# A new table of steps, and later constants issued behind the first query, in a software-pipelined graph attention + Mamba2 + GRU + MoE kernel

## The chip, the cores and the metric

The kernel runs on one core of one Trainium2 chip. The core has five engines that work side by side, each on its own instructions in order: PE (TensorE, matrix products, with its weight loads listed apart as PEld), DVE (VectorE), ACT (ScalarE), POOL (GpSimd) and SP (SyncE, which here only issues DMAs). They wait for each other through semaphores. The metric is the device time of one execution in microseconds (us), as the median of several runs.

## The reference, cut to what matters

The input is `x` of 32 elements x 512 tokens x 256 features and, for each element, an adjacency matrix of 512 x 512. All arithmetic is in 32-bit floats. Two layers are computed, each with a residual sum:

```python
# layer 0
x = x + gat(layernorm(x), adj, W, a)        # leaky_relu(f1_i + f2_j), mask, softmax, times W h
x = x + mamba2_block(layernorm(x), ...)     # x @ W_in, conv of 4, silu, scan over time, gate, norm, W_out, W_lin
# layer 1
x = x + gru_cell(gat1(adj, layernorm(x)), layernorm(x))
x = x + moe(layernorm(x))                   # shared MLP + the best 2 of 4 experts
```

In the attention, the score of a pair of tokens depends on one number of each of the two tokens (`f1`, `f2`). No step mixes two elements.

## The kernel before, in words

One element is 4 tiles of 128 tokens (T=4). The work on one element is cut into 21 parts, listed in `PARTS`: `load_x`, `load_adj`, `gnn0` (the attention of layer 0), `mamba` (its layer norm), `steps_of_time`, `decays_of_states`, two halves of `convolution`, `products_of_bc`, `gate_of_z`, `scan`, `output`, `load_adj` again, `gnn1` (the attention of layer 1), two halves of `gru` (m=0 and m=1), `gru_out`, `moe`, `gates`, `experts` and `mixture`. Each part is a Python generator: it issues a few instructions, yields, and goes on at its next turn.

What sets the order of all instructions is a table written out by hand, `PLAN`: for each part, the turn of each of its steps. Element b adds b times `PERIOD` (428) to its turns; all steps of all elements are sorted by turn and issued in that order, and no scheduler changes it afterwards. 428 is also the number of steps of one element, so a turn is a place in the order and not a time. In the steady state some four to five elements are in flight: while `gnn0` of one element runs, `scan` of the element before, `gnn1` and `gru` of one further ahead and `experts` of another are interleaved with it. Each engine takes its own instructions strictly in that order; so an instruction that waits holds up everything behind it on its engine.

The names that matter below:

- `attention` (L277 on; used by `gnn0` and `gnn1`): DVE takes the largest `f2` (`top`), PE transposes it (`ps_top`, L287), DVE and ACT make 8 rows of factors `fewT` (L300, L302), SP writes them to DRAM as `line` (L305) and reads them back, spread over all partitions, as `query` (L308, 512 KB). ACT (L320) and DVE (L323, L326, with the adjacency tile `adj`) turn `query` into the unnormalised scores `pT`, two tiles at a time. PE multiplies them in `gnn0` (`ps_h`, L356) or `gnn1` (`ps_g`, L692).
- The issuing of DMAs: all of them are issued by SP, in one queue. At the start the constants are loaded: the tables of layer 0 first, then those of later parts from `woutT` (L130) to `gb`. Inside the loop, SP issues per element the loads of `x` and twice of four `adj` tiles, `rows` and twelve `ecs` for the scan, `gates` and four `pg` for the experts, `line` and `query` of both attentions, and the output. Eight semaphores are used in turn for DMAs, so a DMA also waits for the eighth before it.
- `steps_of_time`: PE sums the decays (`ps_E`, L441), DVE makes `byS`, `byL` and `byHL` (L444, L446, L456), PE multiplies these (`ps_seg`, L464), ACT makes the decay tables `L` (L470, L473).
- `gru`: PE sums two products for each gate (`ps_rz`, L718 and L721), and `ps_hn` and `ps_in` (L743); ACT makes `gate`, POOL subtracts (L751, both operands 128x512), DVE finishes with L753 and L755 (`oT`). `gru_out` has PE transpose `oT` (`ps_o`, L764), and DVE adds it to `x`.
- `mamba`: after the layer norm, POOL adds `blin` to `x` (L376, 128x1024). `output` sums squares (L653, `ps_ss` L665) and multiplies with `wc`, a product of `woutT` and `wlin` that is made once, by `prepare_output` (L215 on), ahead of the first element's `output`. That preparation is the first user of the constants of later parts.

Of the kernel before, what the change touches and what calls it, by code (L numbers as in the profile page):

```python
# [11 lines left out]
F32 = mybir.dt.float32  # L12
# [6 lines left out]
P = 128  # L19
N = 512  # L20
T = N // P
D = 256
KD = D // P
HEADS = 8
NP = HEADS // 2
HD = 64
# [5 lines left out]
def adj_ffn_kernel(ctx: ExitStack, tc: tile.TileContext, i: dict, out: bass.AP):  # L32
    nc = tc.nc
# [47 lines left out]
    def load(name, shape, src):  # L81
        t_ = const.tile(shape, F32, name=name)
        nc.sync.dma_start(t_, src)
        return t_

    def kchunks(ap):
        return ap.rearrange("(k p) o -> p k o", p=P)
# [18 lines left out]

    we = const.tile([P, KD, D + 1], F32, name="we")
    nc.sync.dma_start(we[:, :, :D], kchunks(i["L0_gnn_W"]))  # L110
    first = Element(0)
# [14 lines left out]
    dskip = load("dskip", [P, NP], i["dskip"])  # L126
    normw = load("normw", [P, NP], i["norm_w"])
    blin = load("blin", [P, D], i["L0_ffn_b_lin"].partition_broadcast(P))
    woutT = quad("woutT", KD)
    nc.sync.dma_start(woutT, kchunks(i["woutT"]))  # L130
    wlin = row("wlin").rearrange("p (k d) -> p k d", k=KD)
    nc.sync.dma_start(wlin, kchunks(i["L0_ffn_W_lin"]))
    w1 = row("w1").rearrange("p (k d) -> p k d", k=KD)
    nc.sync.dma_start(w1, kchunks(i["L1_gnn_W"]))
    nc.sync.dma_start(abs_[1], i["L1_gnn_a"].partition_broadcast(P))
    wT = row("wT").rearrange("p (k d) -> p k d", k=KD)
    nc.sync.dma_start(wT, kchunks(i["L1_gnn_WT"]))
    raw = big("raw").rearrange("p t n -> p (t n)")[:, :KD * 3 * D].rearrange("p (k o) -> p k o", k=KD)
    nc.sync.dma_start(raw, kchunks(i["wihT"]))
    whh = load("whh", [P, KD, 3 * D], kchunks(i["whhT"]))  # L140
    bih = load("bih", [P, 6], i["b_ih"])
    bhh = load("bhh", [P, 6], i["b_hh"])
    sw1 = load("sw1", [P, KD, 256], kchunks(i["L1_ffn_sW1"]))
    sb1 = load("sb1", [P, 2], i["sb1"])
    sw2 = load("sw2", [P, 2, P], kchunks(i["L1_ffn_sW2"]))
    sb2 = load("sb2", [P, 1], i["sb2"])
    sw3 = load("sw3", [P, D], i["L1_ffn_sW3"])
    ew1 = const.tile([P, KD, 4, P], F32, name="ew1")
    for e in range(4):
        nc.sync.dma_start(ew1[:, :, e, :], kchunks(i["L1_ffn_eW1"][e]))  # L150
    eb1 = load("eb1", [P, 4], i["eb1"])
    ew2 = load("ew2", [P, 4, HD], i["L1_ffn_eW2"].rearrange("e f g -> f e g"))
    eb2 = load("eb2", [P, 2], i["eb2"])
    ew3 = load("ew3", [P, 2, D], i["ew3"].rearrange("(j p) o -> p j o", p=P))
    b3 = const.tile([P, D], F32, name="b3")
    nc.gpsimd.memset(b3, 0.0)
    for r in range(0, P, 32):
        nc.sync.dma_start(b3[r:r + 4, :], i["L1_ffn_eb3"])
        nc.sync.dma_start(b3[r + 4:r + 5, :], i["L1_ffn_sb3"].unsqueeze(0))
    gw = const.tile([P, KD, 32], F32, name="gw")  # L160
    nc.gpsimd.memset(gw, 0.0)
    nc.sync.dma_start(gw[:, :, :4], kchunks(i["L1_ffn_gW"]))
    gb = load("gb", [P, 4], i["L1_ffn_gb"].partition_broadcast(P))


    slopes = const.tile([P, 3], F32, name="slopes")
# [111 lines left out]
    def attention(e, f21, kind):  # L278

        f2 = f21[:, 0, :]
        top = small.tile([P, 1], F32, name="top")
        nc.vector.tensor_reduce(top, f2, AX.X, ALU.max)
        yield
        pt = bank("ps_top")
        nc.tensor.transpose(pt[:, :P], top.to_broadcast([P, P]), ident)  # L287
        yield
        nf = small.tile([P, 1], F32, name="nf")
        nc.vector.tensor_reduce(nf, pt[:, :P], AX.X, ALU.max, negate=True)  # L290
        yield
        nfs = small.tile([P, 2], F32, name="nfs")
        nc.vector.tensor_scalar_mul(nfs, slopes[:, 0:3:2], nf)
        yield

        pf = bank("ps_f1")
        nc.tensor.transpose(pf[:2 * T, :P], f21[:, 1:, :].rearrange("p u t -> p (u t)"), ident)
        yield
        q8 = small.tile([P, P], F32, name="fewT", bufs=4)[:2 * T, :]
        nc.scalar.activation(q8, pf[:2 * T, :P], AF.Relu, scale=slopes[:2 * T, 1:2], bias=nfs[:2 * T, 1:2])  # L300
        yield
        nc.scalar.activation(q8, q8, AF.Exp, scale=-1.0)  # L302
        yield
        line = dram.tile([2 * T, P], F32, name="line")
        nc.sync.dma_start(line, q8)  # L305
        yield
        query = quad("query", 2)
        nc.sync.dma_start(query.rearrange("p n (t m) -> p (n t) m", t=T), line.partition_broadcast(P))  # L308
        yield
        key1 = small.tile([P, T], F32, name="key1")  # L310
        nc.scalar.activation(key1, f2, AF.Exp, bias=nf)
        key2 = small.tile([P, T], F32, name="key2")
        nc.scalar.activation(key2, f2, AF.Exp, scale=0.2, bias=nfs[:, 0:1])
        yield
        pT = big("pT")

        for j in range(0, T, 2):
            both = [(i, pT[:, i, :]) for i in (j, j + 1)]
            for i, p in both:
                nc.scalar.activation(p, query[:, 0, :], AF.Identity, scale=key1[:, i:i + 1])  # L320
                yield
            for i, p in both:
                nc.vector.scalar_tensor_tensor(p, query[:, 1, :], key2[:, i:i + 1], p, op0=ALU.mult, op1=ALU.max)  # L323
                yield
            for i, p in both:
                nc.vector.scalar_tensor_tensor(p, e.adj[i].bitcast(kind), 2.0 ** -120, p, op0=ALU.max, op1=ALU.min)  # L326
                yield
        return pT
# [558 lines left out]
    def mixture(e):  # L887
# [10 lines left out]
        for t, ps in enumerate(pes):  # L898
# [17 lines left out]

    PERIOD = 428
    PLAN = (
        (51,),
        (0, 99, 106, 135),  # L920
        (82, 83, 84, 86, 87, 88, 89, 91, 101, 102, 110, 111, 113, 114, 118, 119, 120, 121, 131, 138, 139, 144,
         147, 151, 152, 153, 158, 159, 160, 161, 162, 194, 196, 203, 204, 205, 206, 207, 208, 210, 211, 212,
         223, 249, 250, 251, 261, 262, 263, 276, 277, 278, 279, 280, 281, 282, 284, 289, 290, 291, 295),
        (283, 287, 292, 297, 298, 300, 314, 315, 316, 317, 325, 354, 355, 356, 357, 409),
        (525, 526, 532, 545, 551, 552, 595, 596, 597, 598, 599, 600, 601, 602, 603, 604, 605, 614, 616, 617,
         618, 625, 626, 627, 628, 629, 660, 661, 662, 663, 664, 665, 666, 667, 668, 669, 670, 671, 672, 673,
         674, 675, 721, 724),
        (630, 637, 722),
        (381, 382, 383, 384, 394, 395, 398, 412, 413, 457, 462, 464, 467, 469, 470, 476, 477, 480, 485, 518,
         591),  # L930
        (414, 415, 463, 465, 466, 478, 501, 502, 506, 513, 522, 523, 540, 676),
        (425, 426, 543, 555, 556, 557, 558, 583),
        (385, 389, 396, 427, 447, 473, 475, 488, 507, 508, 568, 576),
        (684, 685, 686, 687, 688, 694, 695, 696, 697, 698, 699, 700, 701, 702, 703, 727, 729, 730, 731, 732,
         733, 735, 737, 738, 739, 740, 749, 754, 755, 756, 757, 758, 759, 760, 761, 763, 764, 786, 787),
        (734, 741, 746, 747, 762, 765, 766, 767, 775, 776, 788, 789, 790, 791, 792, 793, 794, 795, 796, 797,
         807, 808, 819, 820, 821, 828, 829, 830, 831, 833, 834, 836, 838, 844),
        (736, 781, 889, 902),
        (285, 832, 835, 839, 845, 846, 847, 848, 857, 858, 859, 860, 861, 862, 863, 864, 865, 866, 867, 868,
         869, 870, 871, 872, 873, 874, 878, 879, 880, 881, 882, 883, 886, 910, 911, 914, 915, 919, 920, 921,  # L940
         922, 923, 924, 925, 926, 927, 928, 931, 932, 933, 937, 948, 949, 959, 961, 965, 972, 981, 982, 989,
         990, 992, 993),
        (909, 917, 918, 1021, 1022, 1034, 1035, 1047, 1048, 1049, 1073, 1074, 1075, 1082, 1083),
        (896, 900, 912, 1013, 1036, 1039, 1040, 1043, 1051, 1077, 1078, 1080, 1085, 1086, 1087),
        (1108, 1109, 1110, 1120),
        (1111, 1121, 1200, 1201, 1206, 1207, 1208, 1226, 1227, 1228, 1229, 1242, 1243, 1244, 1246),
        (1384, 1391, 1416, 1425, 1426, 1427, 1430, 1434, 1438, 1440, 1465, 1466, 1469, 1497, 1498, 1499, 1500,
         1504, 1509, 1512, 1570, 1572, 1624, 1630, 1662),
        (1327, 1380, 1392, 1406, 1429, 1433, 1604, 1606, 1607, 1608, 1625, 1626, 1627, 1633, 1658, 1659, 1660,
         1661),  # L950
        (1681, 1683, 1705, 1706, 1707, 1708, 1732, 1733, 1740, 1743, 1744, 1876),
    )
    order = sorted((b * PERIOD + turn, b, n, k) for b in range(B) for n, turns in enumerate(PLAN)
                   for k, turn in enumerate(turns) if b or n > 1)
# [55 lines left out]
```

## Time and profile before

| what | us |
|---|---|
| median of 3 runs | 3426.61 (3424.37 to 3428.89) |
| profiled execution, its own time | 3430.65 |
| span of the profiled execution | 3428.9 |
| PE busy in the span | 3281.2 (96%) |
| DVE busy | 2917.6 (85%) |
| ACT busy | 1527.9 (45%) |
| POOL busy | 543.4 (16%) |
| one steady period (distance at which PE's groups repeat) | 102.75 |
| PE busy in the first 50 us, in the next 50, in the next 100 | 9.58, 33.02, 87.10 |

The span is the time between the first and the last instruction of the profiled execution; its own time has 1.75 us more around it. The mean granted clock of PE is 0.992. The 32 elements at 102.75 us would be 3288 us; the rest is the filling of the pipeline at the start and its draining at the end. Busy shares are means over the whole span[...].

### The profile page before, as it was taken

What the parts mean: (1) busy time and instruction counts of PE and PEld (TensorE: products, weight loads), DVE (VectorE), ACT (ScalarE), POOL (GpSimd) and SP (SyncE); (2) the same over time, 40 slices, a digit from 0 to 9 for tenths busy, and PEclk for the clock granted to TensorE, in tenths of its full rate; (3) what the DMA queues carried; (4) which work ended last, traced back from release to release, by engine and by line L of the source; (5) the groups of instructions that cost most, each with busy time, mean ns of one, the idle gap of its engine ahead of it and who ended that gap; (6) DMA issues with size and microseconds to landing.
All of it is one profiled execution on the core that took longest, in us unless ns stands there. A gap on an engine that the chain in (4) does not pass through costs nothing.

```text
span 3428.9 us, 48462 instructions
## 1 busy us (share of the span) xinstructions
PE 3281.2 (96%) x16616; PEld 1920.2 (56%) x16616; DVE 2917.6 (85%) x7650; ACT 1527.9 (45%) x3016; POOL 543.4 (16%) x591
## 2 busy tenths in 40 slices
PE   4789999999999999999999999999999999999988
PEld 2455556555556555556555556555556555556554
DVE  4788888988888888888888888988888988888963
ACT  2344444444444444444444444444444444444432
POOL 0111111111111111111111111111111111111110
PEclk9899999999999999999999999999999999999999
DMA  3101111212111212111212111212111212111111
GB/s 120 49 31 61 55 57 51 67 39 67 55 56 51 67 39 67 54 56 52 67 39 67 54 56 51 67 39 67 55 57 49 67 39 67 56 58 48 55 32 37
DMA packets 187983, 190.41 MB, mean 56 GB/s; under 512 B 18884, under 2 KB 145496, under 8 KB 187736
## 3 DMA queue, kind: packets, MB, share of 16 engines
q1 hardware_dynamic: 187736, 187.31, 18.0%
q8 instruction: 132, 2.16, 0.3%
q14 instruction: 115, 0.94, 0.1%
HBM read 166.01 MB, written 21.23 MB: 55 GB/s over the span
## 4 chain that ended last, share of the span: by engine, by line
PE 76%; DVE 11%; issue 6%; DMA 4%; ACT 2%; SPq 1%; POOL 0%; DVEq 0%; ACTq 0%; POOLq 0%
PE ps_g L692 7%; PE ps_e L864 6%; PE ps_conv L493 6%; PE ps_mo L674 6%; PE ps_z L555 5%; PE ps_rz L721 4%; DMA query<-line 4%; PE ps_rz L718 3%; PE ps_y L629 3%; PE ps_h L356 3%; PE ps_in L743 3%; DVE pT L323 3%; PE ps_g L364 3%; PE ps_e L902 3%; PE ps_xT L273 2%
## 5 line engine op out<-in xcount | busy, mean ns | idle before, releaser
L500 DVE SCALAR_TENSOR_TENSOR acc<-ps_conv,cw,acc 128x511 f32<-128x511 f32 (+2 forms) x480 | 348.9, 744 | 16.4 <-ACT acc L497 10.6
L245 POOL TENSOR_TENSOR rstd<-rstd,mhalf 128x4 f32<-128x4 f32 x128 | 129.4, 1011 | 1194.8 <-DVE rstd L243 1038.9
L323 DVE SCALAR_TENSOR_TENSOR pT<-query,key,pT 128x512 f32<-128x512 f32 x256 | 213.9, 876 | 107.9 <-ACT pT L320 107.9
L493 PE MATMUL ps_conv<-xT,win 128*128 128x512 f32 x640 | 300.9, 601 | 0.0
L692 PE MATMUL ps_g<-xn,pT 128*128 128x257 f32 x1024 | 259.9, 392 | 12.4 <-DVE pT L326 12.2
L356 PE MATMUL ps_h<-pT,xn 128*128 128x512 f32 x512 | 237.0, 607 | 23.3 <-DVE pT L326 23.3
L596 POOL TENSOR_TENSOR ecs<-ecs,cc 128x512 f32<-128x512 f32 x96 | 134.0, 1396 | 770.3 <-DVE rs L368 531.0
L692 PEld LDWEIGHTS ps_g<-xn,pT 128*128 128x128 f32 x1024 | 190.4, 192 | 100.4 <-issue 33.9
L555 PE MATMUL ps_z<-xT,win 128*128 128x512 f32 x512 | 242.3, 596 | 0.0
L721 PE MATMUL ps_rz<-go,wih 128*128 128x512 f32 x512 | 238.7, 599 | 0.0
L320 ACT ACTIVATE pT<-query,key 128x512 f32<-128x512 f32 x256 | 172.3, 710 | 148.0 <-DMA query<-line 148.0
L864 PE MATMUL ps_e<-xT,ew 128*128 128x512 f32 x512 | 237.0, 596 | 0.0
L718 PE MATMUL ps_rz<-xT,whh 128*128 128x512 f32 x512 | 235.4, 592 | 0.0
L674 PE MATMUL ps_mo<-wc,xh 128*128 128x256 f32 x1024 | 227.2, 380 | 0.0
L497 ACT ACTIVATE acc<-ps_conv,cb,cw 128x512 f32<-128x512 f32 x160 | 123.9, 774 | 220.8 <-PE ps_conv L493 220.7
L262 DVE TENSOR_SCALAR xn<-x,mv,rstd 128x256 f32<-128x256 f32 (+1 forms) x512 | 215.3, 474 | 6.0 <-POOL rstd L245 5.9
L255 DVE BATCH_NORM_STATS2 st<-x 128x6 f32<-128x256 f32 x512 | 206.2, 420 | 6.6
L674 PEld LDWEIGHTS ps_mo<-wc,xh 128*128 128x128 f32 x1024 | 193.1, 191 | 24.8
L849 ACT ACTIVATE e<-ps_e,eb 128x512 f32<-128x512 f32 x192 | 127.6, 680 | 176.7 <-PE ps_e L864 174.7
L751 POOL TENSOR_TENSOR oT<-xT,gate 128x512 f32<-128x512 f32 x64 | 112.4, 1778 | 581.7 <-ACT gate L748 581.7
L493 PEld LDWEIGHTS ps_conv<-xT,win 128*128 128x128 f32 x640 | 120.2, 192 | 149.3 <-issue 142.7
L657 ACT ACTIVATE sq<-xh 128x512 f32<-128x512 f32 x128 | 79.9, 631 | 255.1 <-DVE xh L653 253.7
(205 smaller groups left out, 6691.6 us busy)
## 6 DMA issues: line engine op xcount, KB each, us to landing
adj<-in_adjT_dram SPq DMA_DIRECT2D x256, 256.0 KB
query<-line SPq DMA_DIRECT2D x64, 512.0 KB
ecs<-rows SPq DMA_DIRECT2D x384, 64.0 KB
x<-in_x_dram SPq DMA_DIRECT2D x32, 512.0 KB
pg<-gates SPq DMA_DIRECT2D x128, 128.0 KB
out_dram<-x SPq DMA_DIRECT2D x32, 512.0 KB
rows<-fewT SPq DMA_DIRECT2D x32, 64.0 KB
gates<-fewT SPq DMA_DIRECT2D x32, 64.0 KB
```

The source lines that it names most:

```text
L255: nc.vector.bn_stats(st[:, t, :], x[:, t, :])
L262: nc.vector.tensor_scalar(xn[:, t, :width], x[:, t, :width], mv[:, t, 0:1], r[:, t:t + 1], op0=ALU.subtract, op1=ALU.mult)
L323: nc.vector.scalar_tensor_tensor(p, query[:, 1, :], key2[:, i:i + 1], p, op0=ALU.mult, op1=ALU.max)
L356: nc.tensor.matmul(ps, xn[:, j, k * P:(k + 1) * P], pT[:, j, :], start=j == 0, stop=j == T - 1)
L493: nc.tensor.matmul(ps, win[:, k, 512 + c * P:512 + (c + 1) * P], e.xT[:, k, :], start=k == 0, stop=k == KD - 1)
L500: nc.vector.scalar_tensor_tensor(acc[:, s:], ps[:, :N - s], cw[:, c, 3 - s:4 - s], acc[:, s:], op0=ALU.mult, op1=ALU.add)
L555: nc.tensor.matmul(ps, win[:, k, j * P:(j + 1) * P], uT[:, k, :], start=k == 0, stop=k == KD - 1)
L674: nc.tensor.matmul(ps[:, :D], xh[:, j, t * P:(t + 1) * P], wc[:, j, :], start=j == 0, stop=j == NP - 1)
L692: nc.tensor.matmul(ps[:, :D + 1], pT[:, j, cut], xn[:, j, :], start=j == 0, stop=j == T - 1)
L718: nc.tensor.matmul(ps, whh[:, k, cols], xT[:, k, :], start=k == 0, stop=False)
L721: nc.tensor.matmul(ps, wih[:, k, cols], e.go[:, k, :], start=False, stop=k == KD - 1)
L864: nc.tensor.matmul(ps, ew1[:, k, m, :], vT[:, k, :], start=k == 0, stop=k == KD - 1)
```

## The change

Two things are changed. First, 31 DMAs that load the constants of later parts are no longer issued at the start: `load_later` and `tile_later` only note them on a list, and `attention` issues that list for the first element, directly behind its `query`. Their tiles, sizes and sources stay as they were; together they carry about 4.5 MB. Second, the turns in `PLAN` are new. `PERIOD`, the parts and the number of their steps stay; an element's last turn is 1954 in place of 1876.

```diff
+    later = []
+
+    def load_later(t_, src):
+        later.append((t_, src))
+
+    def tile_later(name, shape, src):
+        t_ = const.tile(shape, F32, name=name)
+        load_later(t_, src)
+        return t_
+
     woutT = quad("woutT", KD)
-    nc.sync.dma_start(woutT, kchunks(i["woutT"]))
+    load_later(woutT, kchunks(i["woutT"]))
...
-    whh = load("whh", [P, KD, 3 * D], kchunks(i["whhT"]))
-    bih = load("bih", [P, 6], i["b_ih"])
+    whh = tile_later("whh", [P, KD, 3 * D], kchunks(i["whhT"]))
+    bih = tile_later("bih", [P, 6], i["b_ih"])
...
-    nc.sync.dma_start(gw[:, :, :4], kchunks(i["L1_ffn_gW"]))
-    gb = load("gb", [P, 4], i["L1_ffn_gb"].partition_broadcast(P))
+    load_later(gw[:, :, :4], kchunks(i["L1_ffn_gW"]))
+    gb = tile_later("gb", [P, 4], i["L1_ffn_gb"].partition_broadcast(P))
...
         nc.sync.dma_start(query.rearrange("p n (t m) -> p (n t) m", t=T), line.partition_broadcast(P))
+        if e is first:
+            while later:
+                nc.sync.dma_start(*later.pop(0))
         yield
```

Of the new table, the rows that are spoken of below (in the order of `PARTS`: `load_x` and `load_adj`, then the second `load_adj`, the two halves of `gru` and `gru_out`):

```diff
-        (51,),
-        (0, 99, 106, 135),
+        (100,),
+        (0, 156, 169, 206),
...
-        (736, 781, 889, 902),
+        (854, 867, 923, 925),
...
-        (909, 917, 918, 1021, 1022, 1034, 1035, 1047, 1048, 1049, 1073, 1074, 1075, 1082, 1083),
-        (896, 900, 912, 1013, 1036, 1039, 1040, 1043, 1051, 1077, 1078, 1080, 1085, 1086, 1087),
-        (1108, 1109, 1110, 1120),
+        (983, 984, 985, 1115, 1116, 1120, 1121, 1122, 1162, 1189, 1207, 1208, 1222, 1223, 1224),
+        (980, 990, 991, 1094, 1095, 1097, 1099, 1100, 1101, 1136, 1137, 1138, 1139, 1140, 1142),
+        (1251, 1252, 1253, 1254),
```

In SP's queue the steady order per element changes with it. Before: `rows`, 12 `ecs`, `adj`, `gates`, 2 `pg`, `adj`, 2 `pg`, `adj`, `line` of `gnn1`, 2 `adj`, `x`, `query` of `gnn1`, 3 `adj`, `line` and `query` of `gnn0`, output. After: `rows`, 12 `ecs`, 3 `adj`, `gates`, 4 `pg`, 2 `adj`, `x`, `line` and `query` of `gnn1`, 3 `adj`, `line` and `query` of `gnn0`, output. Of the two halves of `gru`, before has them interleaved step by step on PE; after finishes m=1 first, and the last gate of m=0 comes later, behind steps of `experts` and `scan` of other elements.

Lines of the changed kernel are numbered one higher from L110 on, 11 higher behind the constants, and 14 higher from L322 on.

## The prediction

> **What bounds the kernel now.** I read the page's busy times and slices first, then the table by stretches of time, then the timeline of the start, the waits, and one period of the timeline in the middle. The page:
>
> ```profile
> PE 3281.2 (96%) x16616; PEld 1920.2 (56%) x16616; DVE 2917.6 (85%) x7650; ACT 1527.9 (45%) x3016; POOL 543.4 (16%) x591
> PE   4789999999999999999999999999999999999988
> DVE  4788888988888888888888888988888988888963
> DMA  3101111212111212111212111212111212111111
> ```
>
> TensorE is busy nearly always, except in the first three slices (85.7 us each) and a little in the last two. The table by stretches says how much (columns after the length: busy us of PE, PEld, DVE, ACT, POOL; granted clock; DMA share; GB/s):
>
> ```profile
> 0.00:50.00 50.00, 9.58 (x19) 4.22 (x20) 15.61 (x57) 6.15 (x11) 3.81 (x18) 1.00 0.64 206
> 50.00:100.00 50.00, 33.02 (x120) 15.91 (x120) 38.36 (x110) 20.02 (x40) 4.60 (x5) 0.81 0.05 14
> 100.00:200.00 100.00, 87.10 (x414) 52.25 (x413) 72.98 (x198) 35.05 (x70) 11.97 (x13) 0.92 0.14 44
> 428.00:856.00 428.00, 421.98 (x2208) 246.98 (x2207) 380.41 (x995) 195.53 (x386) 73.63 (x77) 1.00 0.19 56
> ```
>
> The reader is to see two regimes. In the middle an element costs 102.75 us (the distance after which TensorE's groups repeat), PE busy 98.6% of it: only a shorter or longer hand-off on TensorE's own path counts there, some 29 times over. In the first 200 us PE lacks 70 us; each microsecond by which the first element's chain starts earlier is worth up to one, once. The start in the timeline (start, length; in brackets the idle time before and what ended it):
>
> ```profile
> 20.15 0.31 ACT L302 ACTIVATE fewT<-fewT 8x128 f32<-8x128 f32 x1
> 33.06 0.47 SPq L83 DMA_DIRECT2D gb<-in_L_ffn_gb_dram  x1
> 33.63 0.29 SPq L305 DMA_DIRECT2D line<-fewT  x1
> 35.28 0.34 SPq L308 DMA_DIRECT2D query<-line  x1
> 39.63 2.56 ACT L320 ACTIVATE pT<-query,key 128x512 f32<-128x512 f32 x4 [18.79 <-DMA query<-line]
> 42.46 9.26 PE L356 MATMUL ps_h<-pT,xn 128*128 128x512 f32 x16 [23.27 <-DVE pT L326]
> ```
>
> ACT had the query factors ready at 20.46 us (L302), but SP's queue is in order and still issues constants up to `gb` at 33.06; only then go `line` and `query`, and ACT, DVE and PE stand idle for 19 to 23 us. The waits (total us, times, longest) show the same, and the small stalls of the middle:
>
> ```profile
> ACT pT L320 <- DMA query<-line: 148.0, 34, 18.8
> PE ps_h L356 <- DVE pT L326: 23.3, 1, 23.3
> PE ps_o L764 <- DVE oT L755: 32.6, 31, 2.2
> ```
>
> The first wait happens once per element, but 34 times make 148.0 us, and ACT is 45% busy; only the first, of 18.8 us, passes on to PE (second row). The third is PE's own, about 1.05 us per element. One period's timeline shows its origin:
>
> ```profile
> 1638.41 0.42 PE L441 MATMUL ps_E<-le,dA 128*32 128x128 f32 x8
> 1638.91 0.41 DVE L444 TENSOR_SCALAR byS<-ps_E,kinds 128x128 f32<-128x128 f32 x1 [0.32 <-PE ps_E L441]
> 1639.48 3.49 POOL L751 TENSOR_TENSOR oT<-xT,gate 128x512 f32<-128x512 f32 x2 [16.64 <-ACT gate L748]
> 1639.67 2.16 DVE L456 TENSOR_TENSOR byHL<-byL,head 128x1024 f32<-128x1024 f32 x1
> 1644.12 2.00 PE L464 MATMUL ps_seg<-byHL,byS 32*128 32x512 f32 x16
> 1646.05 3.70 PE L356 MATMUL ps_h<-pT,xn 128*128 128x512 f32 x8
> 1651.39 0.98 PE L764 MATMUL ps_o<-ident,oT 128*128 128x128 f32 x7 [1.02 <-DVE oT L755]
> ```
>
> From the start of `ps_h` to that of the last group is 5.34 us; eight matmuls at 0.43 (the spacing of 512-column records) and one transposition of 0.11 fill 3.55. So the hand-off costs 1.8 us per element. DVE is late because, between `byS` and L755, it has some 10.6 us of work and loses two more to POOL's subtraction (next part).
>
> **What the Trainium skill says.** "SBUF — State Buffer", section "Who interferes with whom": a DVE instruction with two SBUF inputs contends with a GpSimd one that reads SBUF, and the one that came first gets the shared ports for its whole length. The trace agrees: `byHL` takes 2.16 us beside POOL's L751 above, and 1.22 at the shortest of its 32 instances; L890, typically 0.69, takes 2.79 when POOL's L376 (2.35 us) has begun. "DMA: Bandwidth & Descriptors", section "Issuing engines are not separate DMA queues": all transfers run on the same 16 engines, so constants issued behind the query still share them with it if they overtake. The trace: share 0.64 in the first 50 us, 0.19 in the middle. What the two small transfers cost, the trace has itself, from element 1: `line` 89.18 to `query` 90.41 (1.23 us), and `query` to ACT's first use 94.14 (3.73). "Perfetto Trace Analysis", section "Identifying the Most-Contended Engine": matmul busy time is a poor measure of nearness to the limit, because matmuls are pipelined. It agrees: at the fastest spacings seen, an element's TensorE work is 97.5 to 98 us, so 98.6% busy still hides about 5 us of slack per element.
>
> **The change, part by part.**
>
> *Constants behind the query.* 31 DMAs (`woutT` to `gb`, issued 13.81 to 33.53 in before) move behind `query`. The last load that stays, `blin`, is issued at about 11.3, and the first element's arithmetic up to L302 needs none of the moved ones. So `line` goes at about 20.5 (end of L302), `query` 1.23 later at 21.8, ACT's L320 3.73 to 4.35 later (element 1's and element 0's own spacing): 25.5 to 26.1 against 39.63. Gain 13.5 to 14.1 us; I take 13.5. No work on PE covers this idle time, and everything after it in the first element hangs on it. What is late next: (1) the moved constants themselves. They took 19.7 us to issue, so they will be out at about 42 and landed by about 50; the first user is the preparation of `output` (L215) at 115 us, later 101: 50 us of cover. (2) Element 1's `adj` and `x`, behind them in SP's queue: issued at about 43 to 46 instead of 36 to 38, first used by DVE's statistics at 78.10, later about 64.6: 15 us of cover. (3) Bandwidth: the query is issued first, so at worst a part of a microsecond. If PE were saturated in the next 150 us the gain would be eaten; it is idle for 17 us in 50:100 and 13 in 100:200, so I expect it to pass on whole. Bounds: −14.5 to −10.
>
> *`query` of the second attention directly behind `line`.* In before, two `adj` and `x` stand between: for element 0 `line` 162.64, `query` 164.43, use at 171.99, that is 9.35 us, and PE stands about 4 us at `ps_g` 171 to 177. In after, by the order of the two programs, they follow each other: 1.23+3.73 = 5.0 us. Saves 4.4 us of the chain in the fill; part will show as another wait. I take −3 (0 to −5). In the middle of the run this transfer has slack: the wait stands on ACT; PE's share (`ps_g` on DVE's `pT`, 12.2 us in total over 18 times) is 0.4 per element and goes.
>
> *The new table, steady part.* It adds and removes no instruction; it changes positions. On TensorE, before has E, four gate groups (5.2 us), `ps_seg`, `ps_h`, `ps_o`; after puts `ps_o` far behind the last gate, so the 1.8 us goes. Together with `ps_g`: −2.2 us. New, by adding row durations along the new order:
> - From `ps_top` to dA DVE has 5.6 us of steps, TensorE 5.2 to 5.4 of other work: with 0.3 for the hand-over, a stall of about 0.65 ahead of `ps_E`.
> - Between `ps_E` and `ps_seg` TensorE now has only one gate and one `in` group, 3.4 us, in place of 5.2. DVE needs `byS`, `byL`, `byHL`: 0.41+0.40+1.22 and hand-overs. If it is free, 0.15 stall; if POOL's L751 (it becomes ready within 0.1 us of `byHL`) takes the ports first, `byHL` is held, 1.2. I weigh the second 0.7: about 0.9.
> - POOL's L376 now falls beside L755 and L653 of another element, and holds DVE about 2.2 us; with TensorE's work in front of `ps_ss`, 0.8 of it arrives (0.3 to 1.5).
>
> Sum: −2.2 +0.65 +0.9 +0.8 = +0.15 us per element, in truth 0 with an error of 0.7. Over 29 steady elements 0 ± 20 us. Both ends: −1.2 (no collision) to +1.5 (both).
>
> *The end.* An element's own chain becomes 59 places of the order longer (turn 1876 to 1954), which is a depth of places, not time: the last element's chain at the end has 40 us of PE idle in the last 250 us in before. After, a stall of 2.2 us ahead of the gates goes (two more groups stand in front), and a longer run from `pg` to the next matmul costs 1 to 2. I take 0 (−3 to +5).
>
> The sum, against the profiled execution: 3430.65 (span 3428.90 and 1.75 around it) − 13.5 − 3 + 0 + 0 = 3414.2. The median of the runs shown, 3426.61, stands 4.0 below that execution; so 3410, and with the steady +0.15 rounded in part, 3411.
>
> **The rivals.** (B) *Steady shorter too*, by 0.5 to 1.2 us per element: the `ps_o` stall goes and POOL starts its operations at moments when DVE isn't reading two inputs. For it: the gain is visible in two rows of waits. Against: POOL's operations become ready at places where DVE's chains are short of time. It gives 3411 − 29×(0.5 to 1.2) = 3376 to 3396. (C) *Slower side*: the new hand-off ahead of `ps_seg`. POOL's L751 takes the shared ports first in every period, `byHL` waits for it, and with only 3.4 us of TensorE work in front, each such hold is lost whole; L376 adds its own. It turns at 16/29 = 0.55 us per element: beyond that the fill's 16.5 us are used up. At +1.0 it gives 3411+29 = 3440, at +1.5 3454. For it: `byHL` is held already today (2.16 instead of 1.22), hidden by 5.2 us of gates. Against: it needs POOL to win each time by 0.1 us. (D) *The fill gain doesn't arrive*: the constants or element 1's loads come late, or the time is taken back by PE's full queue: then 3424 to 3427, no change. Against: the covers of 15 and 50 us above.
>
> **How the numbers follow.** Forecast A (steady within 0.5 us per element, fill gain arrives): 0.48, own range 3396 to 3426. B 0.25, C 0.22, D 0.05. About 0.2%, 6.9 us, is what a measurement of this kernel can tell from no change: faster is below 3419.8, slower above 3433.5. From A 0.41 are faster and 0.07 within; B is all faster; of C 0.08 are within and 0.14 slower; D is within, 0.04, or slower, 0.01. Sum: 0.66, 0.19, 0.15. For the range, B's lower end beyond 3384 (0.05) and C's beyond 3440 (0.10) are left out, and so it holds some 0.85.
>
> **What would show it.** The timeline of after: `line` at about 20.5, `query` at 21.8, ACT's L334 at 25.5 to 26.1; PE's first `ps_h` at about 29; `x` of element 1 used near 64.6 without a wait on its DMA. The waits: `ps_o` on DVE gone; in its place `ps_E` or `ps_seg` on DVE, and the mean of `byHL` above 1.3 or not, which decides between B and C. The period: 102.75 ± 0.5. Wrong if `query` is used later than 30 us, if the period moves by more than 0.7, or if the last 250 us lose more than 5.

## The result, and the profile after

The changed kernel takes 3459.68 us (median of 4 runs, 3458.51 to 3463.68) against 3426.53 of before in the same session (4 runs): the ratio is 1.0099, with a 95% interval of 1.0081 to 1.0116. It is slower by 33 us; the forecast was 3411, faster. The profiled execution took 3458.51 us, its span is 3456.8. One of the 13 runs of `e5_copy_early` below, 3819.31 us at a granted clock of 0.847, is left out of every comparison.

I read the page again first, then the table by stretches (length; busy us of PE, PEld, DVE, ACT, POOL; clock; DMA share; GB/s):

```profile
PE 3283.0 (95%) x16616; PEld 1912.2 (55%) x16616; DVE 2870.3 (83%) x7650; ACT 1536.0 (44%) x3016; POOL 577.5 (17%) x591
```

```profile
0.00:50.00 50.00, 19.28 (x49) 9.78 (x50) 21.29 (x82) 8.02 (x15) 7.24 (x21) 0.97 0.64 206
50.00:100.00 50.00, 37.95 (x192) 19.64 (x191) 42.12 (x112) 24.51 (x48) 3.33 (x4) 0.82 0.21 66
100.00:200.00 100.00, 91.43 (x479) 53.94 (x477) 85.38 (x224) 43.35 (x85) 19.49 (x18) 1.00 0.13 41
428.00:856.00 428.00, 415.39 (x2111) 243.53 (x2110) 366.12 (x978) 191.85 (x378) 74.23 (x75) 1.00 0.18 54
```

PE's work is the same (3283.0 against 3281.2 us busy). What moved is its idle time. The fill, the first stretch in which the elements enter the pipeline, is much better: 19.28 and 37.95 us busy in the first two stretches against 9.58 and 33.02. The middle is worse: 415.39 of 428 us against 421.98. Written as PE's idle time, from the same table over three stretches:

| PE idle, us | before | after | difference |
|---|---|---|---|
| 0 to 428 | 84.1 | 63.9 | -20.2 |
| 428 to 3200 | 41.6 | 85.7 | +44.1 |
| 3200 to the end | 21.9 | 24.2 | +2.3 |
| PE busy in the whole span | 3281.2 | 3283.0 | +1.8 |

The sum is +28.0, and the spans differ by 27.9. The stretches are stretches of time, not of work: the changed kernel is further back in its work at 3200 us. The distance between two elements' `ps_E`, the period, is 104.75 us, in before 102.76 (here and below the mean from the sixth element to the twenty-eighth): 2.0 us more per element. The start did what it was forecast to do (timeline: start, length, idle time before with what ended it):

```profile
20.25 0.31 ACT L313 ACTIVATE fewT<-fewT 8x128 f32<-8x128 f32 x1
20.58 0.35 SPq L316 DMA_DIRECT2D line<-fewT  x1
21.82 0.35 SPq L319 DMA_DIRECT2D query<-line  x1
26.12 2.56 ACT L334 ACTIVATE pT<-query,key 128x512 f32<-128x512 f32 x4 [5.19 <-DMA query<-line]
28.95 9.47 PE L370 MATMUL ps_h<-pT,xn 128*128 128x512 f32 x16 [9.66 <-DVE pT L340]
42.67 0.47 SPq L322 DMA_DIRECT2D gb<-in_L_ffn_gb_dram  x1
```

`line`, `query`, ACT's first use and PE's first product are each 13.0 to 13.5 us earlier, and the last constant now leaves at 42.67 (the list holds 32 DMAs by the trace, not 31). So the loss is in the middle. PE's waits in the changed kernel (us in total, times, longest), and one of DVE's:

```profile
PE ps_gT L840 <- DVE fewT L837: 29.3, 30, 1.0
PE ps_seg L478 <- DVE byHL L470: 25.6, 27, 2.2
PE ps_ss L679 <- DVE sq L675: 22.3, 34, 2.6
PE ps_mo L688 <- DVE ms L681: 20.1, 20, 2.1
...
PE ps_y L651 <- POOL ecs L610: 7.8, 31, 1.3
```

```profile
DVE e L904 <- DMA pg<-gates: 56.6, 30, 8.0
```

`ps_o` on DVE, 32.6 us in before, happens once, for 3.3 us, and `ps_g` on `pT` (12.2) is gone. Five others have come or grown, 105 us in all. In the middle, from 428 to 3200 us, these five are all the waits that PE has, 85.0 us of its 85.7 of idle time:

```profile
PE ps_gT L840 <- DVE fewT L837: 26.0, 26, 1.0
PE ps_seg L478 <- DVE byHL L470: 19.8, 22, 1.1
PE ps_mo L688 <- DVE ms L681: 19.8, 19, 2.1
PE ps_ss L679 <- DVE sq L675: 14.0, 26, 0.5
PE ps_y L651 <- POOL ecs L610: 5.4, 26, 0.2
```

In before it has three in the same stretch, 41.4 of 41.6 us:

```profile
PE ps_o L764 <- DVE oT L755: 27.6, 27, 1.0
PE ps_o L764 <- DVE fewT L823: 9.2, 27, 0.4
PE ps_g L692 <- DVE pT L326: 4.6, 11, 0.9
```

Two timelines of one period show where the new ones are from. First around `ps_seg`:

```profile
1523.05 0.43 PE L455 MATMUL ps_E<-le,dA 128*32 128x128 f32 x8
...
1525.49 1.29 POOL L765 TENSOR_TENSOR oT<-xT,gate 128x512 f32<-128x512 f32 x1 [29.10 <-ACT gate L762]
...
1525.54 2.32 DVE L470 TENSOR_TENSOR byHL<-byL,head 128x1024 f32<-128x1024 f32 x1
...
1528.00 1.14 PE L478 MATMUL ps_seg<-byHL,byS 32*128 32x512 f32 x8 [0.90 <-DVE byHL L470]
```

POOL's subtraction starts 0.05 us before `byHL`, which takes 2.32 us instead of 1.22, and PE waits 0.90. Then the next 23 us, from the addition of `blin` (POOL L390) on:

```profile
1556.37 2.73 POOL L390 TENSOR_TENSOR x<-x,blin 128x1024 f32<-128x1024 f32 x1 [1.05 <-DVE xn L273]
...
1556.93 2.72 DVE L769 SCALAR_TENSOR_TENSOR oT<-oT,gate 128x512 f32<-128x512 f32 x1
...
1559.77 0.17 DVE L837 TENSOR_TENSOR fewT<-lg,red 128x16 f32<-128x16 f32 x1
...
1560.00 0.33 PE L840 MATMUL ps_gT<-ident,fewT 128*128 128x128 f32 x1 [1.02 <-DVE fewT L837]
...
1563.43 1.31 ACT L671 ACTIVATE sq<-xh 128x512 f32<-128x512 f32 x2 [3.72 <-DVE xh L667]
...
1564.64 0.25 ACT L843 COPY fewT<-ps_gT 128x128 f32<-128x128 f32 x1
...
1566.47 0.41 PE L679 MATMUL ps_ss<-ident,sq 128*128 128x128 f32 x2 [0.54 <-DVE sq L675]
1566.49 2.58 SPq L855 DMA_DIRECT2D pg<-gates  x4
```

```profile
1577.07 0.69 DVE L904 TENSOR_TENSOR e<-e,pg 128x512 f32<-128x512 f32 x1 [1.27 <-DMA pg<-gates]
...
1578.34 0.41 DVE L681 TENSOR_REDUCE ms<-ps_ss 128x2 f32<-128x256 f32 x1
...
1578.80 3.72 PE L688 MATMUL ps_mo<-wc,xh 128*128 128x256 f32 x16 [0.38 <-DVE ms L681]
```

DVE's L769 has two inputs of 128x512 and takes 2.72 us where 0.69 is usual; L390 has begun 0.56 us before it. Everything behind it on DVE is late: `fewT` (L837), and with it `ps_gT`; later `sq`, and with it `ps_ss`. A second chain begins at `ps_gT`: ACT copies it only at 1564.64, because in ACT's order two squarings stand ahead, for which ACT waits 3.72 us. So `gates` and `pg` are issued late, DVE stands at L904 until the second `pg` has landed, `ms` comes behind it, and PE waits for `ms` with the second half of `ps_mo`. `ps_mo` reads nothing that `ms` makes. By the program what it waits for is the PSUM bank of `ps_ss`, one of eight, which `ms` sets free; that last link is read from the program and not tested apart.

### The profile page after: what moved, and what is told of

Read it like the earlier page. It is cut to its first block, busy times and chain, and to the rows that moved or that the text cites. A ratio compares the mean times of both kernels' runs of the same rounds, so it can differ in the third digit from the quotient of the medians.

```text
span 3456.8 us, 48397 instructions
## 1 busy us (share of the span) xinstructions
PE 3283.0 (95%) x16616; PEld 1912.2 (55%) x16616; DVE 2870.3 (83%) x7650; ACT 1536.0 (44%) x3016; POOL 577.5 (17%) x591
## 4 chain that ended last, share of the span: by engine, by line
PE 61%; DVE 25%; DMA 7%; issue 4%; SPq 1%; ACT 0%; DVEq 0%; POOL 0%; POOLq 0%; ACTq 0%
PE ps_g L706 7%; PE ps_h L370 6%; PE ps_z L569 6%; DMA pg<-gates 6%; PE ps_rz L732 6%; PE ps_conv L507 5%; PE ps_mo L688 4%; PE ps_e L916 3%; PE ps_hn L745 3%; PE ps_s L869 3%; DVE oT L769 2%; PE ps_rz L735 2%; PE ps_seg L478 2%; DVE L L589 2%; PE ps_e L878 2%
## 5 line engine op out<-in xcount | busy, mean ns | idle before, releaser
L256 POOL TENSOR_TENSOR rstd<-rstd,mhalf 128x4 f32<-128x4 f32 x128 | 184.9, 1445 | 921.7 <-DVE rstd L254 921.7
L688 PE MATMUL ps_mo<-wc,xh 128*128 128x256 f32 x1024 | 233.6, 383 | 20.2 <-DVE ms L681 20.1
L706 PE MATMUL ps_g<-xn,pT 128*128 128x257 f32 x1024 | 246.5, 383 | 0.0
L765 POOL TENSOR_TENSOR oT<-xT,gate 128x512 f32<-128x512 f32 x64 | 85.8, 1340 | 955.9 <-ACT gate L762 897.1
L732 PE MATMUL ps_rz<-xT,whh 128*128 128x512 f32 x512 | 244.2, 600 | 0.0
L738 ACT ACTIVATE gate<-ps_rz,brz 128x512 f32<-128x512 f32 x128 | 87.8, 686 | 336.0 <-PE ps_rz L735 336.0
L370 PE MATMUL ps_h<-pT,xn 128*128 128x512 f32 x512 | 227.5, 597 | 9.7 <-DVE pT L340 9.7
L337 DVE SCALAR_TENSOR_TENSOR pT<-query,key,pT 128x512 f32<-128x512 f32 x256 | 187.5, 763 | 13.4 <-ACT pT L334 13.4
L266 DVE BATCH_NORM_STATS2 st<-x 128x6 f32<-128x256 f32 x512 | 191.3, 416 | 2.2
L571 ACT ACTIVATE sz<-ps_z 128x512 f32<-128x512 f32 x128 | 75.0, 586 | 261.8 <-PE ps_z L569 261.8
L350 DVE SCALAR_TENSOR_TENSOR prod<-xn,wrow 128x256 f32<-128x256 f32 x512 | 183.5, 420 | 0.0
```

The source lines that it names most:

```text
L266: nc.vector.bn_stats(st[:, t, :], x[:, t, :])
L370: nc.tensor.matmul(ps, xn[:, j, k * P:(k + 1) * P], pT[:, j, :], start=j == 0, stop=j == T - 1)
L688: nc.tensor.matmul(ps[:, :D], xh[:, j, t * P:(t + 1) * P], wc[:, j, :], start=j == 0, stop=j == NP - 1)
L706: nc.tensor.matmul(ps[:, :D + 1], pT[:, j, cut], xn[:, j, :], start=j == 0, stop=j == T - 1)
L732: nc.tensor.matmul(ps, whh[:, k, cols], xT[:, k, :], start=k == 0, stop=False)
```

## The experiments

Three theories stood against each other. One: the start and the table are two things, and in the table each new wait of PE is a hand-off of its own, with its own price. Two: the new order leaves DVE without slack, so that a stall removed in one place comes back in the next. Three, the part of the forecast that could still be right: the gain of the fill has the size and the places that were named. Each experiment alters turns in `PLAN` or exchanges the two parts of the change. Those with altered turns move single instructions of POOL, ACT or SP; in their traces PE and DVE issue the same instructions in the same order as the kernel that they start from.

**The two parts apart.**

```diff
 e1: the changed kernel, with the PLAN of before
 e2: the kernel before, with the PLAN of after
```

> The old table with the constants of later parts issued behind the first query. Theory 1 (the start and the table are two separate things; the start gains what it was forecast to gain): query used at about 26 us, 13.5 us less than before, 3413 us. Theory 2 (the time won at the start is given back, because later work of the fill waits for other things): no change, 3424 to 3427.

> The new table with the constants at their old place. Theory 1: after plus the 13.5 us, 3473 us, with the steady period of after, 104.75 us. If the constants only matter in the old table: 3460 us.

e1 took 3413.40 us (ratio to before 0.9966, interval 0.9953 to 0.9978): 12.8 less than before. PE's idle time up to 428 us is 70.2, that is 13.9 less than before, in the middle 41.4 and at the end 21.8, as before. e2 took 3469.52 (1.0130, 1.0117 to 1.0144), 9.8 more than after and 43 more than before, with a period of 104.66 us. The constants behind the query bring 10 to 13 us with either table, so little or nothing of it is given back: the prediction's rival (D) is out. The table costs 43 to 46.

**The addition of `blin` moved.** In the old table it stands directly behind POOL's `rms`; the same place, three POOL instructions later, was given to it in the new one.

```diff
-        (323, 328, 334, 338, 339, 347, 350, 359, 362, 364, 365, 406, 407, 408, 409, 410),
+        (323, 328, 334, 338, 339, 347, 350, 359, 362, 364, 365, 406, 407, 408, 409, 460),
```

> The changed kernel with one turn altered: POOL's addition of blin to x (L390) comes behind POOL's rms of the element's neighbour, where DVE reads PSUM. Theory 1 (each new wait of TensorE is a hand-off of its own, and two of them hang on DVE being held by this addition): the waits ahead of ps_gT (0.95 us per element) and ps_ss (0.7) go, 29 x 1.65 = 48 us less than after, 3412 us; the wait ahead of ps_mo (0.65) may go with them, then 3393. Theory 2 (in the new order DVE is behind anyway, and a stall taken away here appears at the next hand-off): within 10 us of after, 3450 to 3460.

Measured 3396.73 us (0.9918, 0.9904 to 0.9931), 63 less than after. The waits of this kernel:

```profile
PE ps_seg L478 <- DVE byHL L470: 25.5, 27, 2.2
PE ps_mo L688 <- DVE ms L681: 19.1, 18, 2.7
...
PE ps_ss L679 <- DVE sq L675: 13.2, 30, 2.6
```

`ps_gT` falls from 29.3 us to 0.3, `ps_ss` from 22.3 to 13.2, `ps_y` from 7.8 to 3.0; `ps_seg` and `ps_mo` stay. L390 now runs beside DVE's L690, which reads PSUM and one input of SBUF, and neither is held:

```profile
1547.92 2.35 POOL L390 TENSOR_TENSOR x<-x,blin 128x1024 f32<-128x1024 f32 x1
1548.22 1.41 DVE L690 SCALAR_TENSOR_TENSOR x<-ps_mo,rms,x 128x256 f32<-128x256 f32 x3
```

The period is 102.63 us, 2.1 less. The place of this one instruction costs more than the whole table loses (46 us). The gain is above the forecast, since idle time shows only part of a stall (see the last section), and `ps_y` had not been counted.

**The tanh behind L464**, so that POOL's subtraction begins behind `byHL`.

```diff
-        (980, 990, 991, 1094, 1095, 1097, 1099, 1100, 1101, 1136, 1137, 1138, 1139, 1140, 1142),
+        (980, 990, 991, 1094, 1095, 1097, 1099, 1100, 1107, 1136, 1137, 1138, 1139, 1140, 1142),
```

> The changed kernel with one turn altered: ACT's tanh of gru's half m=1 (L762) comes behind ACT's exponential L464, so that POOL's subtraction L765 starts behind DVE's byHL and not just before it. Theory 1: byHL falls from 2.3 to 1.2 us, the wait ahead of ps_seg (0.85 us per element) goes, 29 x 0.85 = 25 us less than after, 3435 us. Theory 2 (the stall moves on): 3455 to 3460.

Measured 3430.47 us (1.0013, 1.0006 to 1.0020), 29 less than after. `byHL` now (ns, shortest/median/longest; in after 1224/2304/2324):

```profile
L470 DVE TENSOR_TENSOR byHL<-byL,head x32: 1224/1225/1227, 79.5 to 3277.8; 128x1024 f32<-128x1024 f32 x32
```

Of the wait ahead of `ps_seg` one instance of 2.2 us is left, from the start of the run; the period is 103.78, 1.0 less. The other waits stand where they stood, but for `ps_mo`, 16.1 us instead of 20.1.

**The copy of `ps_gT` ahead of the squarings.** PE's order stays; ACT's copy moves two instructions forward.

```diff
-         ... 1645, 1653, 1654, 1677, 1678, 1729, 1730, 1731),
+         ... 1645, 1653, 1654, 1673, 1674, 1729, 1730, 1731),
```

> The changed kernel with two turns altered: the transposition ps_gT and above all ACT's copy of it (L843) come ahead of ACT's two squarings L671, for which ACT waits 3.7 us; PE's order stays. Theory 1 (ps_mo waits because DVE stands at L904 for the DMA pg, and pg is late because that copy was issued late): gates and pg are issued 4 us earlier, DVE's wait for pg (56.6 us in all) goes, the wait ahead of ps_mo (0.65 us per element) goes, 29 x 0.65 = 19 us less than after, 3441 us. Theory 2 (ps_mo's wait has another cause, or the stall moves on): 3455 to 3462.

Measured 3429.8 us (1.0011, 1.0002 to 1.0020), 30 less than after. The trace that is read here is that of one more run of the same kernel:

> The same kernel as e5_copy_early, for its trace. Theory 1: DVE's wait for pg (56.6 us in all) and PE's wait ahead of ps_mo (20.1 us) are gone, and about 10 us more of what the earlier copy brought is found at another wait of PE. Theory 2: they are still there, and the time came from elsewhere.

That run took 3431.07 us at a clock of 0.994. PE's list of waits begins:

```profile
PE ps_gT L840 <- DVE fewT L837: 29.6, 30, 1.4
PE ps_seg L478 <- DVE byHL L470: 25.6, 27, 2.2
PE ps_ss L679 <- DVE sq L675: 23.0, 35, 2.6
PE ps_top L298 <- DVE top L295: 18.3, 6, 7.4
```

`ps_mo` has gone from it and DVE's wait for `pg` falls from 56.6 us to 12.6, in 4 places, while the first three waits are those of after. So `ps_mo` did hang on the DMA `pg`, several steps further back. Theory one's guess that 10 us more would show at another wait of PE is wrong, none of the others has shrunk: the period fell by 0.92 us to 103.83, of which 0.65 had shown as idle time ahead of `ps_mo`.

**Two and three of them together.**

> The changed kernel with the addition of blin later and the tanh behind L464. Theory 1: 3459.7 - 63 - 29 = 3368 us. Theory 2 (shared slack): 3385 to 3397.

> The changed kernel with the three alterations together: the addition of blin later, the tanh behind L464, the copy of ps_gT earlier. Theory 1 (separate hand-offs, each with its own price): the addition brought 63 us, the tanh 29, the copy 19 by forecast: 3459.7 - 111 = 3349 us. Theory 2 (they share a slack): no better than the addition alone with part of the others, 3380 to 3397.

The addition and the tanh: 3373.52 us (0.9848, 0.9831 to 0.9864). All three: 3342.62 us (0.9759, 0.9742 to 0.9777), the fastest kernel here, 83 us below before and 117 below after. The single gains, 63, 29 and 30, add up to 122, and together they are 117: the hand-offs are separate to within 5 us (10 by an estimate in the last section). The middle of the three-fold kernel:

```profile
428.00:3200.00 2772.00, 2765.41 (x14187) 1629.24 (x14186) 2386.22 (x6506) 1302.33 (x2588) 475.92 (x487) 1.00 0.19 56
```

PE is idle for 6.6 us in 2772, and the period is 100.96 us, the same within 0.1 for all but a few elements. Theory two falls here: DVE is busy for 86% of that stretch and delivers in time; what is left ahead of `ps_ss` is 6.6 us in the whole stretch. The loss of the change was not the new order as a whole, but three places in it.

**The mirror: the old table with the addition early.** The kernel is e1 with one turn altered.

```diff
-        (283, 287, 292, 297, 298, 300, 314, 315, 316, 317, 325, 354, 355, 356, 357, 409),
+        (283, 287, 292, 297, 298, 300, 314, 315, 316, 317, 325, 354, 355, 356, 357, 358),
```

> The old table with late constants, and one turn altered the other way round: POOL's addition of blin is put directly behind mamba's layer norm, as in the new table, where POOL is idle and DVE is at its two-input squaring sums. Theory 1 (what matters is what DVE is held at, not the table as a whole): DVE is held 2.2 us ahead of ps_ss, and the old table loses as the new one does, 29 x 0.5 to 2.1 us: 3428 to 3475. Theory 2 (the old table has the slack to swallow it): 3410 to 3418.

Measured 3428.49 us (1.0004, 0.9994 to 1.0014), 15 more than e1. The period grows from 102.67 to 103.37 us, and a wait grows that has 1.7 us in 4 places in e1:

```profile
PE ps_ss L679 <- DVE sq L675: 10.8, 32, 2.0
```

The addition now holds another instruction, L667 ahead of `sq`, and not for the expected 2.2 us. The pair of L667 takes 2.29 us here and 1.29 without a hold, so the hold is 1.0:

```profile
1563.07 2.36 POOL L390 TENSOR_TENSOR x<-x,blin 128x1024 f32<-128x1024 f32 x1
1564.28 2.29 DVE L667 TENSOR_TENSOR xh<-xh,sz 128x512 f32<-128x512 f32 x2
```

In the old table as it was, the addition holds DVE as long as in the new one. It holds L890, which takes 0.69 alone:

```profile
1685.78 2.34 POOL L376 TENSOR_TENSOR x<-x,blin 128x1024 f32<-128x1024 f32 x1
1685.89 2.78 DVE L890 TENSOR_TENSOR e<-e,pg 128x512 f32<-128x512 f32 x1
```

Yet none of PE's three waits in the middle of before comes out of it: `ps_o` follows some 65 us later, and `ps_g`'s goes when only the query moves (e9, below), with the hold still there. So a hold of 2.1 us goes with no wait there, one of 1.0 costs 0.7 us per element here, and one of 2.0 costs 2.1 in the new table. The length of the hold does not set its price; what PE waits for behind the held instruction does. No run takes the hold out of the old table altogether.

**The query directly behind its line, in the old table.** The kernel is e1 with the turn of `query` of the second attention moved ahead of two `adj` and `x`.

```diff
-         ... 882, 883, 886, 910, 911, 914, ...
+         ... 882, 883, 886, 887, 911, 914, ...
```

> The old table with late constants, and the query of the second attention directly behind its line in SP's queue, ahead of two adj and x, as in the new table. Theory 1 (this is what the new table gains in the fill, and it takes PE's wait ahead of ps_g away in the steady part): PE's idle time in the first 428 us falls by 3 to 5 us, the wait ahead of ps_g (11.6 us in all) goes, 3413.4 - 15 = 3398 us. Theory 2 (the second attention has slack enough, and the new table's gain in the fill comes from elsewhere): 3410 to 3416, idle time in the first 428 us within 1.5 us of the old table's.

Measured 3390.91 us (0.9898, 0.9882 to 0.9915), 22 less than e1. PE's idle time up to 428 us is 65.8 (428 less the 362.22 below), 4.4 less than in e1, and in the middle 36.7, 4.7 less; `ps_g` on `pT` falls from 11.6 us in 14 places to 2.4 in 2, none of them in the middle, and the period is 102.3 us for every element but the first two and the last, where in e1 it varied between 102.3 and 104.

```profile
0.00:428.00 428.00, 362.22 (x1824) 209.35 (x1825) 351.56 (x932) 177.32 (x347) 66.08 (x83) 0.96 0.21 66
428.00:3200.00 2772.00, 2735.27 (x14031) 1612.16 (x14030) 2462.98 (x6443) 1291.58 (x2543) 461.00 (x490) 1.00 0.18 56
```

Of the 20.2 us that the fill gained in the changed kernel, 13.9 are the constants and 4.4 this; 1.9 stay without a cause.

## Why the prediction was wrong, by its own steps

- *Constants behind the query*: forecast 13.5, measured 13.5 at ACT's first use and 12.8 in e1's median. Right, and so were the covers: no wait on the late constants or on element 1's `x` is in the list.
- *Query behind its line*: forecast -3 in the fill and -0.4 per element, 15 us in all; e9 shows -4.4 in the fill, -0.4 in the period, and 22 us in the median. Right in kind, too small in sum.
- *`ps_o` behind the last gate*: forecast -1.8 per element. Of the 36.8 us that PE stood ahead of `ps_o` in the middle of before nothing is left. Right.
- *`ps_E`*: forecast +0.65. PE waits there once, for 2.9 us. Wrong: the chain from `ps_top` to `dA` keeps up.
- *`ps_seg` held by `byHL`*: forecast +0.9 as a weighted mean. PE waits there 27 times in 32 elements: 0.8 us per element as idle time, 1.0 by the period of e4. Right.
- *POOL's addition*: this is where the sum failed. The prediction said that L376 "holds DVE about 2.2 us; with TensorE's work in front of `ps_ss`, 0.8 of it arrives". The hold is 2.03 us (2.72 less 0.69), as forecast. But the sum followed the held DVE to one reader only. The first instruction behind L755 (L769 in the changed kernel) for which PE waits is not `sq` but `fewT`, for `ps_gT`: 0.95 us per element as idle time. At `ps_ss` less arrives than forecast: moving the addition takes 8.4 us away there in the middle (14.0 to 5.6), 0.3 per element. The addition's whole price is 2.1 us (e3), not 0.8.
- *From `pg` to the next matmul*: the prediction named this run, priced it at 1 to 2 us, and booked it once, in the drain, the last stretch of the run. In the steady part it put the term at nothing, without a reason. There DVE waits 1.8 us per element for `pg`, PE 0.65 for `ms`, and the period loses 0.9 (e5).
- *The end*: forecast 0. Over their last 250 us both kernels have PE busy for the same time, 226.7 us, so this is right; but the idle time there is 23 us and not the 40 that the prediction read, and 1876 to 1954 is 78 places, not 59.

The steady sum, by its own terms: -2.2 + 0 + 1.0 + 2.1 + 0.9 = +1.8; the period grew by 2.0. The first term was not measured as a period. Against the +0.15 of the forecast 1.3 us were missing at the addition, 0.9 at `pg` and 0.1 at `ps_seg`, and 0.65 at `ps_E` was too much: +1.65 us per element, or 48 us in 29 elements. The prediction missed by 49. With the fill 4 us better than its 16.5, the account is closed to about 5 us.

Two of the prediction's own signs against itself came true: the period moved by more than 0.7, and `byHL` stands at 2.30 us, which was to decide for the slower rival. For its 97.5 to 98 us of pure TensorE work in an element no view or run is found; the fastest kernel here has 100.96, with 0.2 us of it idle.

The rival on the slower side named `byHL` held by L751, with L376 adding its own. Its mechanism is there, but `byHL` alone would not have decided: e6 with the 29 us of e4 added would be at 3372 us (an estimate, it was not run), still faster than before. The range ended at +1.0 us per element of this rival, and +2.0 came, because the rival held no hand-off that the sum did not hold already: `ps_gT` and the steady `pg` are in neither.

## What to carry to other kernels

When an order of instructions is changed on an engine-bound kernel, list, for every instruction that can be held, *all* that is queued behind it on its engine up to the next reader of the bounding engine, and not only the reader that one has in mind; and follow each DMA whose issue hangs on an in-order engine from the issuing instruction to the consumer once per period. A slowdown of a new order can be three single places: here three instructions, moved by one to three places on their own engines, took 117 us off, and the new order is then 71 us (2.1%) better than the old one with the same late constants (e1). Read the names in the list of PE's waits first, then ask of each what is ahead of the releaser, the instruction that ended the wait, on *its* engine.

## What the runs showed of the hardware

- The Trainium skill, "SBUF — State Buffer", section "Who interferes with whom", says that a DVE instruction with two SBUF inputs contends with a GpSimd instruction that reads SBUF, that the ports they share are an exclusive lock, and that the order of issue decides who blocks. The runs agree: L769 takes 0.69 alone and 2.72 behind L390, and ends 0.55 us after it; `byHL` takes 1.22 alone and 2.30 behind L765. L390 itself takes 2.73 instead of 2.35 where L767, also with two inputs, was still running when it began. The section also says that a DVE instruction with at most one SBUF input, outside the 2-port modes, does not contend: beside L690 (PSUM and one SBUF input) L390 takes 2.35 us and L690 its usual time.
- A stall of PE costs more than the idle time shown ahead of it. The three single moves took away, as idle time, 1.4 us per element (addition: `ps_gT`, `ps_ss`, `ps_y`), 0.8 (tanh) and 0.65 (copy), and shortened the period by 2.1, 1.0 and 0.9. The rest is in the busy time, which is that of the same 16616 matmuls: 3283.0 us in after, 3255.8 with all three moves.
- With the addition moved, alone or with the tanh, a further cost shows at `ps_mo`. Five times in the middle of these two traces, three in e3 and two in e7, PE's granted clock is 0.5 for 3.4 us, here in e3:

```profile
2166.50:2169.90 3.40, 3.40 (x10) 2.71 (x9) 2.56 (x7) 0.00 (x0) 2.90 (x2) 0.51 0.00 0
```

Each time PE has just waited 2.0 to 2.7 us for `ms`, and no other trace read here has such a stretch in its middle. Waits as long were also passed without it (2.13 us in after, 2.29 in e7), so what decides stays open. By an estimate from these figures each stretch costs 1.7 us, some 5 us in e3, so that the addition's own gain would be rather 68 us than 63.
